# Writing three layers of a graph network as software pipelines in a fixed instruction order

## The chip, the cores and the metric

The kernel runs on one core of one Trainium2 chip. The time is the device time of the core in microseconds (us), median of several executions. "PE" is TensorE's matmul stream, "PEld" its weight loads, "DVE" VectorE, "ACT" ScalarE, "POOL" GpSimd, "SP" SyncE, which only issues transfers. The engines have one queue each and meet through semaphores.

## The reference, cut to what matters

Four graph layers over N = 3327 nodes with D = 512 features and a sparse adjacency; each is `x = layernorm(x + layer(x))`. The sum over neighbours is dense in the reference (`mask @ x`, or a masked softmax):

```python
# layer 0: attention, 8 heads of 64 columns
Wh = einsum('nd,hdo->hno', x, W);  f1 = Wh . a1;  f2 = Wh . a2
e = leaky_relu(f1[:, :, None] + f2[:, None, :], 0.2), masked by adj > 0
x = layernorm(x + elu(softmax(e) @ Wh))
# layer 1: mean over neighbours, two dense products, combined
out = relu(concat(x @ W_self + b_self, (mask @ x / deg) @ W_nb + b_nb) @ W_comb + b_comb)
# layer 2: mean over at most 64 neighbours
xj = leaky_relu(nb_mean @ W_nb.T + b_nb);  xi = leaky_relu(X @ W_line.T + b_line);  out = xi + xj
# layer 3: attention as in layer 0, 4 heads of 128 columns, W expanded as quaternions
```

## The kernel before

The 3327 rows are 26 blocks of 128. For each block the kernel first turns its rows of the adjacency into lists of edges, in chunks of 128 edges: 247 chunks in all, walked in 74 groups of up to four. A layer writes a table of transformed rows to DRAM. For each chunk GpSimd gathers 128 table rows with one indirect transfer (`gt`); VectorE makes a 128 x 128 matrix of zeros and ones that tells which edge belongs to which row (`sel`); TensorE multiplies the two and accumulates the block's sum in PSUM (`acc`). In the attention layers the gathered rows are first multiplied by the edge's weight for each head. After the last chunk of a block comes its end: bias, activation, residual, layernorm (its reciprocal root on GpSimd, `rs`), transposes, and the next layer's dense products.

```python
# attention, one block after the other (cut)
for l, c0, g, at in groups(b):
    G = gather(gp, self.table, l, c0, g, HM + H)
    S = select(sp, l.dst, c0, g)
    ...                                        # scores: one small product per chunk, exp on ScalarE
    for c in range(g):
        nc.vector.tensor_mul(Gh[:, c, :, :OUT], Gh[:, c, :, :OUT], w[:, c, :, None].to_broadcast([P, H, OUT]))
    for c in range(g):
        for s in range(2):
            nc.tensor.matmul(acc[:, s, :hh * M], S[:, c, :], G[:, c, s * hh * M:(s + 1) * hh * M], ...)
...                                            # block end
# layer 1, end of a block (cut)
nc.vector.scalar_tensor_tensor(y, acc, rdeg[b], zb, ALU.mult, ALU.add)
nc.vector.scalar_tensor_tensor(y, y, 0.0, xres[b], ALU.max, ALU.add)
layernorm(fin, y, x2)
xt = transposed(fin, ps, x2)
nc.vector.tensor_add(tb, times(ps, xt, wn2), bn);  store(t2_d, b, tb)
nc.vector.tensor_add(xi, times(ps, xt, wl2, "px"), bl)
...                                            # leaky relu, xres[b] = xi + x2
```

Here the order of instructions on each queue is not the order of this text: an automatic scheduler with a model of durations rearranges them.

## Time and profile before

| | before |
|---|---|
| median | 2683.0 us (4 executions, 2678.6 to 2690.4) |
| TensorE, VectorE, GpSimd busy | 78%, 52%, 40% |
| lengths of the five stages | 318, 827, 555, 496, 493 us |

The stages are cut at the first gather of each layer: projection and weights, then layers 0 to 3. This cut, and the lines under it, are in the prediction below. A row of the table of engines by stage reads: window, its length, then busy us (and number of instructions) of PE, PEld, DVE, ACT, POOL, then the granted TensorE clock as a share of full speed, the busy share of the DMA engines, and GB/s.

### The profile page before, as it was taken

Reading aid. Unit: us, or ns where it says so; the run is one execution under the profiler, and the core shown is the slowest. Engines: PE = TensorE matmul, PEld = TensorE weight load, DVE = VectorE, ACT = ScalarE, POOL = GpSimd, SP = SyncE. Lnnn points to the kernel's source line nnn. Section 1 sums busy time; section 2 is a strip of 40 time slices with the busy share of each in tenths; the row PEclk is TensorE's granted clock in tenths of the full one; section 3 lists DMA queues with packets and bytes.
Section 4 is the critical chain, followed back from the end, with each engine's and each line's share of the span. In section 5 each row is a group of like instructions: output and inputs, shape, how many; then the busy total and the mean of one; then the engine's idle time right before and its main releaser. Section 6 shows DMA issues by size and latency. Waiting matters only on the chain. (4 is left out here: it accounts for less than half of the span.)

```text
span 2688.7 us, 22997 instructions
## 1 busy us (share of the span) xinstructions
PE 2087.9 (78%) x6894; PEld 1234.9 (46%) x6894; DVE 1395.8 (52%) x4087; ACT 408.4 (15%) x913; POOL 1080.5 (40%) x1244
## 2 busy tenths in 40 slices
PE   6697667787878777777888888568888877777775
PEld 3453355565555555423333333123333346666654
DVE  8976155577777774312333443312223336677776
ACT  2124111112222211100000000000111121111111
POOL 1000253433232322176554441565645527556451
PEclk9798988888888887898998998889999988888777
DMA  6136254444554432266554441565544427556442
GB/s 217 61 132 199 72 145 118 118 129 148 166 155 154 140 106 85 65 195 185 157 153 147 139 140 44 151 189 155 163 126 138 142 80 208 153 157 170 134 143 61
DMA packets 127529, 372.23 MB, mean 138 GB/s; under 512 B 25642, under 2 KB 27178, under 8 KB 127396
## 3 DMA queue, kind: packets, MB, share of 16 engines
q0 software_dynamic: 79040, 262.10, 34.6%
q1 hardware_dynamic: 48356, 108.57, 11.8%
q8 instruction: 58, 0.95, 0.2%
q14 instruction: 75, 0.61, 0.1%
HBM read 329.38 MB, written 41.21 MB: 138 GB/s over the span
## 5 line engine op out<-in xcount | busy, mean ns | idle before, releaser
L801 POOL DMA_INDIRECT gt<-t_d,idx x988 | 984.7, 997 | 1024.3 <-issue 331.8
L911 PE MATMUL acc<-gt,sel 128*128 128x260 f32 (+1 forms) x1976 | 626.7, 477 | 250.1 <-DVE gt L907 104.4
L911 PEld LDWEIGHTS acc<-gt,sel 128*128 128x128 f32 x1976 | 456.6, 240 | 356.8 <-ACT gt L905 108.1
L1036 PE MATMUL acc<-gt,sel 128*128 128x512 f32 x988 | 491.7, 627 | 47.4 <-DMA gt<-t_d,idx 46.2
L907 DVE TENSOR_TENSOR gt<-gt,pe 128x512 f32<-128x512 f32 x494 | 317.8, 678 | 13.5 <-ACT pe L904 8.5
L1036 PEld LDWEIGHTS acc<-gt,sel 128*128 128x128 f32 x988 | 178.6, 196 | 284.5 <-issue 208.1
L808 DVE TENSOR_TENSOR sel<-lane,dst 128x384 f32<-128x384 f32 (+2 forms) x284 | 169.0, 595 | 233.5 <-PE acc L1036 142.8
L663 PE MATMUL po<-wn,xt 128*128 128x512 f32 x416 | 219.9, 677 | 7.2 <-ACT xt L657 6.9
L663 PE MATMUL po<-w,xt 128*128 128x512 f32 x416 | 209.3, 643 | 3.0 <-ACT xt L657 3.0
L657 ACT COPY xt<-pt 128x512 f32<-128x512 f32 x112 | 65.6, 586 | 892.6 <-PE pt L655 855.1
L891 ACT ACTIVATE ds<-place,nmid 128x384 f32<-128x384 int16 (+2 forms) x148 | 95.8, 650 | 529.9 <-PE pe L895 524.0
L655 PE MATMUL pt<-s_ident,xres 128*128 128x128 f32 x312 | 59.5, 321 | 120.4 <-DVE xres L674 107.7
L663 PEld LDWEIGHTS po<-wn,xt 128*128 128x128 f32 x416 | 89.8, 223 | 127.4 <-issue 101.1
L685 POOL MEMSET ab<- 128x1 int32 x26 | 2.7, 103 | 349.2 <-ACT m L691 340.8
L663 PEld LDWEIGHTS po<-w,xt 128*128 128x128 f32 x416 | 81.8, 207 | 121.4 <-issue 87.9
L716 DVE MAX8 cand<-val 128x8 f32<-128x832 uint16 (+41 forms) x259 | 127.7, 522 | 0.0
L655 PEld LDWEIGHTS pt<-s_ident,xres 128*128 128x128 f32 x312 | 41.8, 168 | 153.3 <-issue 103.4
L672 POOL TENSOR_SCALAR rs<-mv 128x1 f32<-128x1 f32 x104 | 22.5, 217 | 189.8 <-DVE mv L670 155.3
L663 PE MATMUL px<-wl,xt 128*128 128x512 f32 x208 | 95.7, 603 | 0.8 <-DVE tb L1073 0.8
L691 ACT ACTIVATE m<-ab 128x1664 bf16<-128x1664 int32 x52 | 82.7, 1590 | 80.6 <-DVE val L692 69.3
L663 PE MATMUL po<-wx,xt 128*128 128x512 f32 x208 | 94.6, 597 | 0.0
L674 DVE TENSOR_SCALAR xres<-e,mv,rs 128x512 f32<-128x512 f32 x52 | 30.0, 576 | 124.2 <-POOL rs L673 124.1
(178 smaller groups left out, 2023.8 us busy)
## 6 DMA issues: line engine op xcount, KB each, us to landing
ab<-in_adj_dram SPq DMA_DIRECT2D x25, 832.0 KB, 4.9
ab<-in_adj_dram SPq DMA_DIRECT2D x25, 831.5 KB, 6.1
gt<-t_d,idx POOLq DMA_INDIRECT x988, 3.7
t_d<-tb SPq DMA_DIRECT2D x50, 256.0 KB, 2.0
t_d<-tb SPq DMA_DIRECT2D x25, 264.0 KB, 2.2
t_d<-tb SPq DMA_DIRECT2D x25, 260.0 KB, 2.0
xres<-in_x_dram SPq DMA_DIRECT2D x25, 256.0 KB, 5.7
z_d<-zb SPq DMA_DIRECT2D x25, 256.0 KB, 3.5
```

The source lines that it names most:

```text
L655: nc.tensor.transpose(pt[:, c, :], src[:, c * P:(c + 1) * P], ident)
L657: nc.scalar.copy(xt, pt)
L663: nc.tensor.matmul(po, xt[:, c, :], w[:, c], start=c == 0, stop=c == DC - 1)
L674: nc.vector.tensor_scalar(o, y, mv[:, 0:1], rs, ALU.subtract, ALU.mult)
L691: nc.scalar.activation(m, ab, AF.Sign, accum_out=half[:, s:s + 1])
L716: nc.vector.max(out=top, in_=seg)
L801: nc.gpsimd.indirect_dma_start(out=t[:, c, :], out_offset=None, in_=table[:, :], in_offset=bass.IndirectOffsetOnAxis(ap=l.idx[:, c0 + c:c0 ...
L808: nc.vector.tensor_tensor(s[:, :g, :], lane1[:, None, :].to_broadcast([P, g, P]), which[:, c0:c0 + g, None].to_broadcast([P, g, P]), ALU.i ...
L891: nc.scalar.activation(ds[:, :g * P], place[:, c0 * P:(c0 + g) * P], AF.Abs, bias=l.nmid)
L907: nc.vector.tensor_mul(Gh[:, c, :, :OUT], Gh[:, c, :, :OUT], w[:, c, :, None].to_broadcast([P, H, OUT]))
L911: nc.tensor.matmul(acc[:, s, :hh * M], S[:, c, :], G[:, c, s * hh * M:(s + 1) * hh * M], start=at + c == 0, stop=at + c == last)
L1036: nc.tensor.matmul(acc, S[:, c, :], G[:, c, :], start=at + c == 0, stop=at + c == last)
```

## The change

Its intent is that TensorE never stands for a block's end. Every group and every block end becomes a generator that yields between stages; one step of the loop advances every live generator by one stage, the oldest first, so the stages of some four groups and two blocks are interleaved by hand. From layer 1 on the scheduler is switched off and the queues run in the order written. Cut to its core:

```diff
+class Stages:
+    def step(self):
+        for stages in list(self.live):
+            if next(stages, self) is self:
+                self.live.remove(stages)
...
+        def group(self, item, pools, accs, done):        # attention
+            G = gather(gp, self.table, l, c0, g, H * M)
+            ...
+            yield
+            S = select(sp, l.dst, c0, g)
+            ...                                           # ds, and the score products pe
+            yield
+            ...                                           # sc, exp
+            yield
+            nc.vector.tensor_mul(Gc[:, :, :OUT], Gc[:, :, :OUT], w[:, :g]...)   # one for the group
+            for c in range(g): ... nc.tensor.matmul(accs[b][s], S[:, c, :], G[:, c, ...])
...
+    ctx.enter_context(tc.manual_schedule())               # layers 1 to 3
...
+        def layer1_end(b, acc):
+            yield
+            ...                                           # y from acc, zb, xb; moments -> mv, rs
+            yield
+            scaled(x2, y, mv, rs)
+            xt = transposed(fin, ps, x2)
+            yield
+            nc.vector.tensor_add(tb, times(ps, xt, wn2), bn)
+            store(t2_d, b, tb, 2)
+            yield
+            xi = fin.tile([P, D], F32, name="xi")
+            nc.vector.tensor_add(xi, times(ps, xt, wl2), bl)
+            nc.vector.scalar_tensor_tensor(xi, xi, SAGE_ALPHA, xi, ALU.mult, ALU.max)
+            nc.vector.tensor_add(xres[b], xi, x2)
```

Besides this, the attention table keeps two score columns beside each head's features, so one operation adds both; the list making has fewer small operations; the residual x of layers 0 and 1 is reloaded from DRAM; the preparation of later weights goes into earlier pipelines; and buffers are handed on one by one and not at the ends of pools.

## The prediction

> **What bounds the kernel now.** I read the page first (TensorE 78% busy, VectorE 52%, no engine full), then cut the span at the first gather of each layer, because an average over five different stages says nothing. The table of engine busy time by stage:
>
> ```profile
> 0.00:318.00 318.00, 245.46 (x947) 134.33 (x947) 208.19 (x955) 84.60 (x154) 8.97 (x32) 0.88 0.40 133
> 318.00:1145.00 827.00, 627.70 (x2380) 447.28 (x2380) 523.39 (x1535) 170.84 (x381) 268.16 (x316) 0.83 0.44 129
> 1145.00:1700.00 555.00, 453.19 (x1014) 187.51 (x1014) 195.48 (x341) 15.24 (x26) 267.46 (x301) 0.92 0.47 142
> 1700.00:2196.00 496.00, 405.07 (x1071) 171.23 (x1071) 130.70 (x327) 51.28 (x88) 269.76 (x299) 0.93 0.49 145
> 2196.00:2689.00 493.00, 356.50 (x1484) 294.55 (x1483) 338.00 (x929) 86.41 (x266) 266.14 (x299) 0.79 0.53 148
> ```
>
> Columns: window, its length, then busy us of PE, PEld, DVE, ACT, POOL, then granted clock, DMA share, GB/s. Rows: projection and weights (318 us), layer 0 (827), layer 1 (555), layer 2 (496), layer 3 (493). Layers 0 and 3 are attention, 1 and 2 means over neighbours with dense products. No engine is over 82% in any of them, so order and waits, not work, cost the time. The timeline of layer 1 shows how:
>
> ```profile
> 1400.47 3.70 PE L663 MATMUL po<-wn,xt 128*128 128x512 f32 x8
> ...
> 1419.85 0.61 DVE L674 TENSOR_SCALAR x<-e,mv,rs 128x512 f32<-128x512 f32 x1 [3.96 <-POOL rs L673]
> ...
> 1420.61 1.08 PE L655 MATMUL pt<-s_ident,x 128*128 128x128 f32 x4 [3.36 <-DVE x L674]
> ...
> 1423.19 5.23 PE L663 MATMUL po<-wn,xt 128*128 128x512 f32 x8
> ```
>
> TensorE stood 3.36 us for a block's layernorm, and the same eight passes then took 5.23 us instead of 3.70: it pays for a gap twice, once standing and once at half clock. (The first passes after the gap start 0.85 us apart, warm ones 0.43.) The layer boundaries, and the pace of the gather and of VectorE's weighting, in the same view of other windows:
>
> ```profile
> 317.73 1.18 POOL L801 DMA_INDIRECT gt<-t_d,idx  x1 [67.76 <-DMA t_d<-bias]
> ...
> 1699.68 1.00 POOL L801 DMA_INDIRECT gt<-t_d,idx  x1 [31.64 <-DVE wa L943]
> ...
> 2402.49 3.68 DVE L907 TENSOR_TENSOR gt<-gt,pe 128x512 f32<-128x512 f32 x6
> ...
> 2403.09 0.95 POOL L801 DMA_INDIRECT gt<-t_d,idx  x1 [0.30 <-issue]
> ```
>
> The first attention gather waited 67.76 us for weight products of layer 1 that it does not use; layer 2's waited 31.64 us, the end of it for layer 3's weights. A gather costs POOL 0.95 + 0.30 = 1.25 us a chunk, whatever it waits for. In layer 3 the table of waits carries the same point as layer 1:
>
> ```profile
> PEld acc L911 <- DVE gt L907: 98.8, 58, 6.8
> ```
>
> **What the Trainium skill says.** "TensorE: Matmul & The Clock Gate", Part 1: after an idle window of about 3.4 us the clock halves, and about 3.4 us of sustained work restores it. The trace agrees: 0.85 against 0.43 us a pass after a 3.36 us gap. The section "Back-to-back issue gap" there gives about 216 ns for 512 warm columns; here an f32 product is two records of 0.43 us, so 0.86 us, and the trace decides. "VectorE: DVE Perf Modes", Mode 1x: one f32 result per cycle at 0.96 GHz, so 0.53 us for 512 columns; six products in 3.68 us are 0.60 us each, leaving some 0.07 us to save for every instruction merged away. "DMA: Bandwidth & Descriptors", Issuing engine by pattern: indirect transfers belong to GPSIMD, so the 1.25 us per chunk stays on POOL; the change does not touch it.
>
> **The change, part by part.** The lists hold 42 chunks in block 0 (three lists of 14) and 19, 15, 13, 11, 10, 10, 9, 9, 8, 8, five 7s, eight 6s, two 5s: 247 chunks in 74 groups a layer (988 gathers and 148 activations on the page agree). Per block of L chunks and n groups, warm:
> POOL: 1.26 L + 1 (two small layernorm operations, 0.2 + 0.56 plus gaps), sum 337.
> PE, layer 1: 0.86 L + 7.4 (transposes 0.5, two dense products of 8 x 0.43). PE, layer 2: 0.86 L + 5.7 (one product 3.44, scores 0.9, column mean 0.86, transposes 0.5).
> PE, attention: 1.1 L (four passes of 0.22 for the sum, two of 0.1 for the scores).
> DVE, attention: 0.45 n + 0.73 L + 3.7 (selection 0.06 + 0.13 a chunk, comparison 0.13 + 0.07, scores 0.2, merged weighting 0.06 + 0.53; block end 3.7).
>
> Layers 1 and 2. Each block's tail is cut into stages one group apart, with the sums of later groups between them, so TensorE no longer stands for the layernorm. Taking the larger of PE and POOL block by block gives 416 us for layer 1 (53 of them block 0, where gathers set the pace) and 377 for layer 2. PE alone would be 405 and 361. To each I add start and tail, since the next layer's gathers need every row of the table: some 15 us and 25 us (finishing the scores), and some 20 us for waits that remain: 450 and 420. The preparation of layer 3's weights, some 14 us of VectorE at the end of layer 1 (eight pairs of 0.69 each, and copies), moves into the middle, where VectorE is 35% busy. Saving 105 + 76.
>
> Layer 3. POOL 337, DVE 311, PE 272; larger of them by block 343. All three are close, and POOL must stop for each block's variance before it gathers on, so I expect 50 us of coupling and ends: 395, saving 98. Inside DVE's sum: 494 products become 148 instructions, two layers x 173 x 0.07 = 12 us each; three score operations become two, 74 x 0.16 = 12 us each.
>
> Layer 0 stays with the automatic scheduler, but its order of emission is now staged too. PE work warm: 247 x 1.1 = 272, dense 26 x 7.4 = 192, list products some 40, together 504 where 628 were busy at clock 0.83. DVE: 523, less 24 for attention, less some 30 for the list operations (about eight per list of 0.14 us busy and two per group of slots: 8 x 22 x 0.14 + 5), plus two more structures at some 13 us (fewer fit before the first gather): 495. Two engines near 500 need luck to finish under 600; I take 680, 73% of PE, against 61% of it (504 of 827) now. ACT takes over the copies (41 evacuations and four small operations per list, some 40 us) and has room at 171 of 827. Saving 147.
>
> Projection and weights. PE needs 26 x 5.7 = 147 plus eight weight products and the bias, some 40. They now lie in one pipeline instead of one after the other. Score weights must come first (eight pairs of 0.69 us, 11 us, after a load of 9), so 20 + 187 + finish and first gather 15 + 10 for closing the started structure + some 8 of gaps = 240, saving 78.
>
> Residuals of layers 0 and 1 in DRAM add two stores and loads of 256 KB a block, at 45 to 50% DMA share beside other work: nothing on the path. The final checks go into layer 3's pipeline: 10 us of tail, in its figure.
>
> Sum: 240 + 680 + 450 + 420 + 395 = 2185.
>
> **The rivals.** (1) POOL becomes the bound: at 337 a layer it cannot beat the table above, but if each layernorm pair makes POOL stop some 3 us x 26, layers 2 and 3 lose 60 to 80 each and the end is 2330. For: POOL's waits for the mean and variance already run to 16 us. Against: five or six gather buffers are two groups of lead. (2) The fixed order puts a slow producer ahead of ready work, as a list scheduler would not; then layer 3 stays at 460 and layer 1 at 500: 2310. For: queues are in order. Against: stages are a whole group (3 to 5 us) apart, longer than most handoffs here. (3) Layer 0 is VectorE-bound with single buffers in its list pool and one bank for transposes and list products: 780, so 2290. For: DVE 523 of 827 is spread. (4) TensorE is warm throughout and layer 0 reaches 600: 2080.
>
> **Range.** All parts but layer 0 have waits that are seen and removable; a loss would need the gain of some 500 us to vanish in new waits. Rivals 1 and 3 together give about 2400, rival 4 with good coupling 2060. I state 2185 us, 8 in 10 between 2060 and 2350; faster by over 2% 0.96, same 0.03, slower 0.01.
>
> **What would show it.** The granted clock in layers 1 and 2 near 1 (0.92 and 0.93 now), TensorE's waits for the normalised row nearly gone, gathers of the first layers not waiting for a bias or for score weights, 148 weighting instructions of some 1.9 us, POOL over 75% busy in layer 3. I would be wrong if layer 3 stays above 450 with POOL standing for the variance, or if layer 0 keeps TensorE near clock 0.83 at over 780 us.

## The result, and the profile after

The changed kernel took 2294.4 us (median of 4, 2290.1 to 2298.7) against 2683.0 us, ratio 0.8549, 95% interval 0.8524 to 0.8574. It is clearly faster and inside the range, but 109 us above the number. The engines by stage, in the same columns and the same five stages as before:

```profile
0.00:271.50 271.50, 226.83 (x933) 126.50 (x933) 181.14 (x754) 81.99 (x162) 7.54 (x22) 0.99 0.41 130
271.50:907.50 636.00, 560.66 (x2418) 406.73 (x2419) 518.62 (x1244) 191.42 (x492) 277.85 (x303) 0.91 0.63 195
907.50:1458.90 551.40, 454.65 (x1047) 201.64 (x1045) 193.38 (x339) 20.29 (x35) 274.39 (x302) 0.91 0.53 160
1458.90:1861.00 402.10, 379.81 (x1069) 165.17 (x1069) 126.29 (x330) 47.98 (x81) 266.09 (x299) 0.99 0.61 179
1861.00:2293.50 432.50, 338.03 (x1484) 282.41 (x1484) 348.45 (x687) 81.05 (x246) 269.89 (x327) 0.84 0.59 169
```

| stage | before | predicted | after | after less predicted |
|---|---|---|---|---|
| projection, weights | 318 | 240 | 271.5 | +31 |
| layer 0 | 827 | 680 | 636.0 | -44 |
| layer 1 | 555 | 450 | 551.4 | +101 |
| layer 2 | 496 | 420 | 402.1 | -18 |
| layer 3 | 493 | 395 | 432.5 | +37 |

Layer 1 is the odd row. It was to lose 105 us and lost 4, with its clock still at 0.91, while layer 2, whose block ends are cut into stages too, runs at 0.99. The timeline of layer 1 after the change (start, duration, engine, line, operation, operands; in brackets the idle time of the engine just before and what ended it) shows what TensorE stands for:

```profile
1210.78 3.60 PE L711 MATMUL po<-wl,xt 128*128 128x512 f32 x8
...
1214.41 0.69 DVE L1242 TENSOR_TENSOR xi<-po,bl 128x512 f32<-128x512 f32 x1 [2.41 <-PE po L711]
1215.14 0.69 DVE L1243 SCALAR_TENSOR_TENSOR xi<-xi 128x512 f32<-128x512 f32 x1
1215.86 0.69 DVE L1244 TENSOR_TENSOR xres<-xi,x 128x512 f32<-128x512 f32 x1
1216.47 0.54 DVE L725 TENSOR_SCALAR x<-e,mv,rs 128x512 f32<-128x512 f32 x1
...
1217.16 1.08 PE L703 MATMUL pt<-s_ident,x 128*128 128x128 f32 x4 [2.79 <-DVE x L725]
```

The product with `wl` ends at about 1214.4. VectorE stood 2.41 us for it, then does three operations on it, and only then the `x` of the next block, whose inputs had long been there; TensorE, with nothing before the transposes of that `x` in its queue, stands 2.79 us. The same happens in nearly every block, as the table of waits in layer 1 says (engine, line, what it waited for: us in all, times, longest):

```profile
POOL rs L720 <- DVE mv L718: 179.9, 24, 13.8
...
PE pt L703 <- DVE x L725: 70.3, 25, 3.9
DVE neg L1207 <- DMA raw<-in_L_gnn_W_dram: 29.7, 1, 29.7
```

The other lines of before have these answers. The first gathers of layers 0 and 2 now wait 35.57 us for a list and 11.36 us for the last dense product. The six multiplies of 0.60 us became operations such as the third line, for four chunks at once:

```profile
271.45 1.40 POOL L871 DMA_INDIRECT gt<-t_d,idx  x1 [35.57 <-DVE cand L793]
...
1458.88 1.00 POOL L871 DMA_INDIRECT gt<-t_d,idx  x1 [11.36 <-PE po L711]
...
1965.06 2.27 DVE L971 TENSOR_TENSOR gt<-gt,w 128x2048 f32<-128x2048 f32 x1
```

The wait of the aggregation for the weighting in layer 3, 98.8 us in 58 waits, has no line of that name left. It is not gone, though; part of it stands under another name:

```profile
PEld acc L977 <- issue: 38.1, 42, 2.7
```

"Issue" means that the profile knows nothing that was waited for. But all 40 of these waits that are longer than 0.2 us end 0.07 us after the end of a weighting multiply (L971). So TensorE still stands some 38 us for the weighting.

### The profile page after: what moved, and what is told of

Read it like the earlier page. It is cut to its first block, busy times and chain, and to the rows that moved or that the text cites. A ratio compares the mean times of both kernels' runs of the same rounds, so it can differ in the third digit from the quotient of the medians.

```text
span 2293.5 us, 22330 instructions
## 1 busy us (share of the span) xinstructions
PE 1960.0 (85%) x6950; PEld 1182.5 (52%) x6950; DVE 1367.9 (60%) x3351; ACT 422.7 (18%) x1016; POOL 1095.7 (48%) x1251
## 4 chain that ended last, share of the span: by engine, by line
PE 38%; DVE 9%; DMA 5%; issue 4%; POOL 4%; ACT 1%; SPq 0%; POOLq 0%; DVEq 0%; ACTq 0%
PE acc L1163 16%; PE po L711 12%; PE acc L977 5%; DMA gt<-t_d,idx 4%; POOL gt L871 3%; PE pt L703 1%; PE pe L960 1%; PE pmean L907 1%; DVE h L991 1%; PE pf L893 1%; DVE xi L1243 1%; DVE xi L1242 1%; DVE h L996 1%; DVE x L725 1%; DVE gt L971 1%
## 5 line engine op out<-in xcount | busy, mean ns | idle before, releaser
L977 PE MATMUL acc<-gt,sel 128*128 128x264 f32 (+1 forms) x1976 | 553.9, 436 | 81.2 <-issue 73.5
L977 PEld LDWEIGHTS acc<-gt,sel 128*128 128x128 f32 x1976 | 415.3, 217 | 175.6 <-issue 90.8
L1163 PEld LDWEIGHTS acc<-gt,sel 128*128 128x128 f32 x988 | 192.0, 205 | 267.7 <-issue 205.3
L971 DVE TENSOR_TENSOR gt<-gt,w 128x1536 f32<-128x1536 f32 (+2 forms) x148 | 284.7, 1923 | 1.5 <-ACT w L967 1.3
L878 DVE TENSOR_TENSOR sel<-lane,dst 128x384 f32<-128x384 f32 (+2 forms) x284 | 167.7, 592 | 70.3 <-PE acc L1163 37.4
L711 PE MATMUL po<-wn,xt 128*128 128x512 f32 x416 | 195.7, 612 | 5.6 <-ACT xt L705 5.2
L1237 DVE TENSOR_TENSOR tb<-po,bn 128x512 f32<-128x512 f32 x26 | 18.0, 692 | 204.6 <-PE po L711 204.6
L779 DVE MAX8 cand<-val 128x8 f32<-128x832 uint16 (+39 forms) x259 | 124.3, 521 | 0.0
L703 PE MATMUL pt<-s_ident,x 128*128 128x128 f32 x208 | 38.1, 314 | 82.1 <-DVE x L725 70.8
L960 PE MATMUL pe<-g3fall,ds 128*128 128x8 f32 x494 | 64.8, 254 | 45.0 <-DVE ds L957 45.0
L960 PEld LDWEIGHTS pe<-g3fall,ds 128*128 128x128 f32 x494 | 68.4, 201 | 58.1 <-issue 43.2
L967 ACT ACTIVATE w<-sc 128x24 f32<-128x24 f32 (+4 forms) x148 | 28.2, 191 | 380.0 <-DVE sc L965 267.7
```

The lines of the kernel that those rows point to most:

```text
L703: nc.tensor.transpose(pt[:, c, :], src[:, c * P:(c + 1) * P], ident)
L711: nc.tensor.matmul(po, xt[:, c, :], w[:, c], start=c == 0, stop=c == DC - 1)
L779: nc.vector.max(out=top, in_=seg)
L878: nc.vector.tensor_tensor(s[:, :g, :], lane1[:, None, :].to_broadcast([P, g, P]), which[:, c0:c0 + g, None].to_broadcast([P, g, P]), ALU.i ...
L960: nc.tensor.matmul(pe[:, c], ds[:, c * P:(c + 1) * P], self.fall[:, H:, b], start=True, stop=True)
L971: nc.vector.tensor_mul(Gc[:, :, :OUT], Gc[:, :, :OUT], w[:, :g].rearrange("p c (h o) -> p (c h) o", o=1).to_broadcast([P, g * H, OUT]))
```

## The experiments

My theory after this reading: in a fixed order, a stage that holds a product and the operations of another engine on that product makes the other engine's queue stand for it, and everything behind, though ready, stands too. Rivals: GpSimd's stop for the variance, the 179.9 us above, starves the gathers; the reloaded residuals compete with the gathers; or the clock is a limit of its own.

Twelve kernels ran, in four sets, each set on one chip beside the kernel before. All gave correct results. The chip of the second and fourth sets is slower: the kernel before takes 2728 to 2729 us there against 2685 and 2690 us on the other two, and layer 2, which no edit but e4's touched, 433 to 442 us against 402 to 405. So I compare stages with unedited stages of the same set (where the first set has none, with the changed kernel above, whose layers 0 and 2 agree with those of e1 to e3 within 3 us). Where that chip loses time in layer 3, VectorE's waits for a group's score product and gathered rows show. This is the line of e6:

```profile
DVE sc L964 <- remote: 54.2, 12, 8.5
```

"Remote" is the profile's word for a release that it can assign to no instruction or transfer of the core. In e7 the line reads 53.2 us and in e8 59.7 us; no layer 3 on the other chips has one, and, which matters below, e12's has none either. Without it the unedited layers 3 of the second set would take some 429 and 435 us, as elsewhere.

Lengths of the stages in the profiled executions, edited stages in bold. They come from one execution each; e2's was the fastest of its six, 19 us under the median, and e7's the slowest of its five, 15 us over it:

| run | set | projection | layer 0 | layer 1 | layer 2 | layer 3 | median of all |
|---|---|---|---|---|---|---|---|
| e1_xi_later | 1 | 271.6 | 637.7 | **447.0** | 402.5 | 433.9 | 2193.7 |
| e2_scores_later | 1 | 268.5 | 637.7 | **537.5** | 401.6 | 417.7 | 2284.2 |
| e3_both | 1 | 269.6 | 638.5 | **441.7** | 403.8 | 431.5 | 2190.6 |
| e4_auto | 1 | 271.4 | 642.0 | **445.4** | **412.9** | **464.5** | 2237.3 |
| e5_newest_first | 2 | 271.1 | 646.9 | 558.0 | 437.5 | **742.2** | 2660.6 |
| e6_l0_unstaged | 2 | 271.5 | **705.7** | 557.8 | 433.3 | 483.5 | 2462.3 |
| e7_lists_later | 2 | **249.6** | **661.6** | 557.0 | 441.8 | 488.6 | 2385.5 |
| e8_weight_per_chunk | 2 | 270.9 | **659.3** | 559.5 | 435.4 | **471.6** | 2399.4 |
| c9_control | 3 | 273.4 | 638.6 | 551.5 | 402.8 | 435.3 | 2298.1 |
| e9_best | 3 | **272.8** | 638.8 | **441.3** | 404.0 | **421.7** | 2180.1 |
| e10_more_loads | 3 | **270.6** | **637.3** | **444.2** | 404.8 | **419.3** | 2181.7 |
| e12_vector_relief | 4 | **276.3** | 645.9 | **458.2** | 441.3 | **422.9** | 2245.8 |

**e1_xi_later: the operations on the product one stage later.**

```diff
-            nc.vector.tensor_add(xi, times(ps, xt, wl2), bl)
+            px = times(ps, xt, wl2)
+            yield
+            nc.vector.tensor_add(xi, px, bl)
```

> Only change: in layer 1 the three VectorE operations on wl2's product (bias, leaky relu, sum for layer 2's residual) are written one stage after the product, not in the stage of the product. Theory (a fixed order that puts them, waiting for their own product, ahead of the next block's scaled x makes TensorE wait for x, and the pass after the wait runs cold): TensorE's wait for x in layer 1, 70 us in 25 waits, falls below 15 us, layer 1 goes from 551 to 450-490 us, the whole from 2294 to 2200-2230, nothing else moves. Rival 1 (GpSimd's stop for the variance, 180 us in layer 1, starves the gathers): under 20 us. Rival 2 (residual reloads compete with the gathers for the DMA engines): under 20 us. Rival 3 (the granted clock alone): the gap goes but layer 1 stays above 530 us because the clock falls.

Measured: 2193.7 us (4 executions, 2192.7 to 2199.6), ratio to before 0.8173 (0.8143 to 0.8203) against 0.8549. Layer 1 by engines:

```profile
909.20:1356.20 447.00, 418.62 (x1047) 189.38 (x1045) 194.82 (x339) 20.29 (x35) 272.02 (x301) 0.97 0.65 197
```

And from its table of waits, GpSimd's for the variance and TensorE's for the normalised row:

```profile
POOL rs L720 <- DVE mv L718: 82.7, 21, 9.2
...
PE pt L703 <- DVE x L725: 5.4, 7, 2.9
```

One added `yield` took 104 us from layer 1 and changed the other stages by less than 2 us. The instructions are the same (339 on VectorE, 1047 on TensorE). TensorE's wait for `x` fell from 70.3 to 5.4 us, 65 us; and its busy time fell from 454.65 to 418.62 us, 36 us, because the passes after most of the waits no longer run cold: in the timeline of the changed kernel eight aggregation passes right after one wait took 5.25 us, eight dense ones later 3.60. 65 + 36 = 101 of the 104 us. The rivals fall, as the explanation of this gain: GpSimd's wait for the variance fell by 97 us without being touched. It was the effect, GpSimd ahead and standing for late statistics, not the cause. The clock rose to 0.97 by itself once TensorE had work. That VectorE's queue works strictly first in, first out is stated by the Trainium skill ("TensorE: Matmul & The Clock Gate", "Architectural detail: the array is 16x 32x32, not 1x 128x128"); this pair of runs agrees: `x`, ready behind `xi`, did not pass it.

**e2_scores_later: the weight preparation not ahead of the first selection.** The order also put the first VectorE operation of layer 3's weight preparation (the 29.7 us wait for its transfer, above) ahead of layer 1's first selection.

```diff
-        work.add(score_parts())
-        for item in groups():
+        parts3 = score_parts()
+        next(parts3)
+        for n, item in enumerate(groups()):
+            if n == 12:
+                work.add(parts3)
```

> Only change: layer 3's weight preparation in layer 1's pipeline keeps its load at the start, but its first operation on VectorE is written after 12 groups instead of in the second step, ahead of the first selection. Theory: VectorE's wait of 29.7 us for that load, with TensorE idle behind it at the start of layer 1, goes; layer 1 shortens by 18-28 us, the whole to 2266-2276. Rival (the start of layer 1 waits for the gathers or its own weights anyway): under 8 us.

Measured: 2284.2 us (6 executions, 2264.9 to 2291.6), 10 us less by the medians, with a spread larger than that; layer 1 is 14 us shorter in the profiled run, the fastest of the six. The expectation was too high. TensorE's first aggregation, first in the changed kernel, then here:

```profile
934.91 18.31 PE L1163 MATMUL acc<-gt,sel 128*128 128x512 f32 x36 [6.50 <-DVE sel L878]
```

```profile
926.33 1.09 PE L1193 MATMUL pt<-s_ident,raw 128*128 128x128 f32 x4 [3.60 <-DMA raw<-in_L_gnn_W_line_dram]
927.21 13.21 PE L1163 MATMUL acc<-gt,sel 128*128 128x512 f32 x25
```

With the selection early, TensorE's own queue still holds the transposes of layer 2's weights first, and those wait for their loads until 926.33. Only the 6.50 us and one later wait of 4.25 us were to be had, not VectorE's 29.7. I had read the wait of an engine that was not the last to be ready.

**e3_both: the two edits together.**

> Both edits together. Theory: they are of two separate times and add up: 90-125 us less, the whole 2170-2205, layer 1 430-465 us. If the clock takes it back or the gathers become the bound, less than 70 us together.

Measured: 2190.6 us (2182.6 to 2195.8), ratio 0.8158 (0.8122 to 0.8194): 104 us less than the changed kernel, 3 us less than e1 alone by the medians, 5 us in layer 1. As expected, in the lower half of the range; the second edit adds little.

**e4_auto: the same text, given back to the scheduler.**

```diff
-    ctx.enter_context(tc.manual_schedule())
```

> The changed kernel with the same code, but with layers 1 to 3 given back to the automatic scheduler (one line taken out). It measures what the fixed order itself is worth, in each layer. My theory: the fixed order wins in layers 2 and 3 (402 and 432 us stay below what the scheduler makes of them, by 20-60 us each) and costs in layer 1 (scheduler below 551 us, by 20-80). The whole 2280-2360. Rival (the whole gain of layers 1 to 3 comes from the fixed order): layers 1 to 3 go back to some 1545 us, the whole to 2440.

Measured: 2237.3 us (2236.0 to 2237.8), ratio 0.8329 (0.8301 to 0.8356), 57 us faster than the changed kernel. Layers 1, 2 and 3:

```profile
913.30:1358.70 445.40, 419.12 (x1047) 187.68 (x1045) 184.45 (x309) 20.29 (x35) 276.31 (x301) 0.98 0.62 192
1358.70:1771.60 412.90, 382.62 (x1069) 166.90 (x1069) 128.81 (x330) 50.55 (x82) 269.63 (x299) 0.97 0.60 174
1771.60:2236.10 464.50, 341.37 (x1484) 287.38 (x1484) 320.27 (x686) 85.60 (x245) 261.17 (x327) 0.82 0.55 157
```

The signs are as expected, two of the sizes and the whole are not. The fixed order is worth 10 us in layer 2 (20 to 60 expected) and 31 us in layer 3 (402.5 and 433.9 unedited in e1), and cost 106 us in layer 1 (20 to 80 expected), where the scheduler had moved the tail of a block back against the next: in its timeline an `x` is ready at 1194.9 us and its transposes start at 1205.19 us, without a wait. Against before (555, 496, 493 us) the same text under the scheduler gains 110, 83 and 28 us: as much in layer 1 as the fixed order mended by e1 (108), most of its gain in layer 2 (94) and half in layer 3 (59). That part comes from the staged text and what else the change did there, not from the fixed order.

**e5_newest_first: the other direction of a step, in layer 3.** `step` goes through `list(self.live)[::-1]`.

> The changed kernel, but in layer 3 each step goes through the live pipelines from the newest to the oldest: TensorE's score products stand before the aggregation products, and VectorE makes the next selection before it weights the oldest group. Theory (in layer 3 TensorE's waits for ds, 45 us, and what follows them at a low clock come from the order oldest first): layer 3 goes from 432 to 395-415 us, the whole to 2255-2280. Rival (VectorE, 348 busy of 432 us, is the bound and only start, end and its waits for gathers make up the rest): within 10 us either way.

Measured: 2660.6 us, ratio 0.9747 (0.971 to 0.9785). Layer 3 took 742.2 us where the unedited one of this set takes 483.5 and 488.6. Both the theory and the rival missed by far. The waits of layer 3:

```profile
DVE sel L883 <- PE acc L982: 299.3, 59, 6.8
```

My explanation is argued from the code and this line; no run with more buffers tests it. Selections have three buffers. Oldest first, a step first emits the product that frees a buffer and then the selection that takes it. Newest first, the selection comes ahead and wants the buffer whose product was emitted last in the step before, so VectorE stands for TensorE, then weights, then TensorE runs: the two engines take turns. If that is right, the order of a fixed pipeline and the count of its buffers are one choice, not two.

**e6_l0_unstaged: layer 0 without staging.**

```diff
-        work.add(g0.group(item, pools, accs, layer0))
         more()
+        for stage in g0.group(item, pools, accs, layer0):
+            pass
         work.step()
```

> The changed kernel, but in layer 0 all stages of a group are written together, as the kernel before wrote them, under the same automatic scheduler. Theory (layer 0's gain of 191 us is mostly the staging: gather, scores, weighting and products of four groups written side by side): layer 0 goes from 636 to 740-830 us, the whole to 2400-2490. Rival 1 (the gain comes from cheaper list operations and scores per head, with the order left alone): layer 0 stays under 680. Rival 2 (the merged weighting and the table's layout): the same, under 680.

Measured: 2462.3 us, ratio 0.9042 (0.9009 to 0.9074). Layer 0 is 705.7 us against 646.9 unedited (e5): 59 us. Staging the groups is worth less than I expected, even though the scheduler may reorder: it is a third of the layer's gain of 191 us (which is from another chip). The rest is not split up here beyond e8.

**e7_lists_later: TensorE's first 40 us.** In the changed kernel TensorE's queue had block 0's first list product early, and it stood 39.0 us for it.

```diff
             work.step()
-            more(2)
+            if t >= 3:
+                more(2)
```

> The changed kernel, but the list of block 0 goes on only from the fourth projection block, so that TensorE has three blocks' transposes and products in its queue ahead of the first list product, for which it now waits 39 us (the scheduler put that product early in TensorE's order). Theory (the projection stage is bound by TensorE, 227 busy of 271 us, and lost its first 40 us to that wait): projection 271 to 245-258 us, the whole 12-26 us less. Rival (VectorE's lists set the end of the stage, so a later start only moves the wait to the end, before the first gather): within 6 us either way or longer.

Measured: 2385.5 us, ratio 0.8745 (0.8724 to 0.8765). The projection stage fell to 249.6 us, as expected, but fewer lists were done by then, and layer 0 rose to 661.6: together 911.2 against 918.0 in e5. A saving of some 7 us, where 12 to 26 were expected of the whole; the list work had moved across the border.

**e8_weight_per_chunk: the weighting not merged.** The one multiply per group becomes a loop over its chunks.

> The changed kernel, but the features are weighted chunk by chunk again: 494 multiplies of 512 columns in place of 148 of up to four chunks, about 33 us more of VectorE over layers 0 and 3 going by the two profiles (317.8 against 284.7 us). Theory: layer 3 is bound by VectorE and takes all of its half, some 15 us; layer 0 has slack on VectorE (519 of 636 us) and takes 0-8. The whole 12-28 us more. Rival: hidden, under 5 us.

Measured: 2399.4 us, ratio 0.8798 (0.8774 to 0.8821). Against the unedited stages of the set, layer 0 is 12 us longer (659.3 against 646.9, where 0 to 8 were expected) and layer 3 is 12 to 17 us shorter (471.6 against 483.5 and 488.6). Layer 3, its VectorE 10 us busier:

```profile
1925.10:2396.70 471.60, 337.12 (x1484) 281.39 (x1484) 356.92 (x859) 81.26 (x246) 270.71 (x327) 0.83 0.54 155
```

My expectation failed for layer 3. The likely reason is that TensorE can start on the first chunk after 0.6 us and need not wait for the whole 1.9 us operation; a merge that saves VectorE's time lengthens the hand-over. The traces bear this out: the waits `PEld acc L977 <- issue` come to 6.2 us here, and to 34.6 and 35.2 us in the unedited layers of e6 and e7, and TensorE is busy 337 us for 355 and 353.

**c9_control, e9_best and e10_more_loads.** The control is the changed kernel unedited. The best version joins e3 with two more edits: lists that start late and catch up, and in layer 3 a stage between weighting and product, with the buffers that it needs.

```diff
+            if t >= 3:
+                more(3 if t < 9 else 2)
...
                                  w[:, :g].rearrange("p c (h o) -> p (c h) o", o=1)...)
+            if self.k == 1:
+                yield
...
-        pools = (pool_in(lay, "l3g", 6), pool_in(lay, "l3s", 3),
+        pools = (pool_in(lay, "l3g", 7), pool_in(lay, "l3s", 4),
```

The third loads each residual twice (`for r in range(2)` around the loads of layers 0 and 1).

> The changed kernel itself, unedited, as the control of this chip: the chip of the second set of runs was slower in stages that no edit touched (layer 2 433 to 442 us there, 402 on the first). On a chip like the first: 2285-2300 us. On one like the second: 2370-2410.

> Four edits in four different stages, to be read stage by stage against the control: in layer 1 the two of the first set (xi a stage later; layer 3's weight preparation after 12 groups); in the projection the list of block 0 starts with the fourth block and then catches up in threes; in layer 3 the aggregation product is written one stage after the weighting it reads, with a seventh gather buffer and a fourth selection buffer. Theory (a stage that holds a producer and its consumer on another engine makes the in-order queues wait): layer 3 20-45 us shorter, layer 1 100-115, projection 12-22, layer 2 unchanged, the whole 130-170 us below the control. Rival for layer 3 (VectorE or GpSimd is the bound): layer 3 within 8 us.

> The version before it, but every block's residual is loaded twice: x in layer 0, x1 and z1 in layer 1, so 78 more loads of 256 KB, 20 MB more. Theory (the reloads lie beside other work; DMA engines are busy 0.65 of layer 1): each of the two layers within 6 us, the whole within 10. Rival (they compete with the gathers now that layer 1 is bound by TensorE and the gathers): layer 1 15-40 us longer.

Measured: control 2298.1 us (2294.6 to 2303.3), ratio 0.8546 (0.8507 to 0.8585), as on the first chip. Best version 2180.1 us (6 executions, 2176.5 to 2186.1), ratio 0.8112 (0.8082 to 0.8142): 118 us below the control, less than the 130 to 170 I expected. With doubled loads 2181.7 us, ratio 0.8122 (0.8084 to 0.8159). By stages: layer 1 551.5 to 441.3 us, confirmed on one chip. Projection unchanged: TensorE has its first work at 14.87 us and is busy 237 us, for 230 in the control, but stands later in the stage for the lists that now come late. Layer 3 435.3 to 421.7, 14 us, between theory and rival: TensorE's waits right behind the weighting went from 38 to 2 us, but those for `ds` rose from 44.2 to 71.6 us. Of the fixed order, the three executions with this stage (e9, e10, e12) took 419 to 423 us and four without it on the fast chips 431 to 435; but one without it, e2's, took 417.7, so 14 us are not more than one execution can vary. The doubled loads, 20 MB more, cost layer 1 3 us and layer 0 nothing (637.3 against 638.8), although layer 1's DMA share rose from 0.65 to 0.72: the reload is hidden, and the rival that blamed it falls. (Only the loads were doubled, not the store.)

**e12_vector_relief: less VectorE work in layer 3.** In e9's layer 3 VectorE is 84 to 94% busy, window by window, from 103 us after its start to 39 us before its end. The edit weights the last chunk of groups of three or four on ScalarE, and forms the exponential linear unit as min(exp(h), 1) in the sum.

```diff
+            gv = g - 1 if self.k == 1 and g >= 3 else g
...
+            for h in range(H if gv < g else 0):
+                cols = G[:, gv, h * M:h * M + OUT]
+                nc.scalar.mul(cols, cols, w[:, gv, h:h + 1])
```

> The best version so far, with VectorE relieved in layer 3 alone: the last chunk of each group of three or four is weighted on ScalarE (four scalings of 128 columns), and the exponential linear unit takes the smaller of exp(h) and 1 in the sum (one operation of 0.45 us per block less). About 70 x 0.53 + 26 x 0.45 = 49 us of VectorE less of 346; ScalarE gains some 280 x 0.25 = 70 us on 81. Theory (once the products are a stage later, VectorE is the bound of layer 3's middle: 84 to 94% busy in its windows from 103 us on): layer 3 goes from 422 to 385-405 us. Rival (GpSimd's gathers and TensorE's low clock hold it): within 8 us of 420. On a chip as slow as the second set's: compare with its layer 3 of 471 to 487 us and its layer 2 of 433 to 442.

Measured: 2245.8 us (6 executions, 2240.5 to 2249.4), ratio 0.8222 (0.8198 to 0.8247), on the slow chip. Layers 2 and 3:

```profile
1380.40:1821.70 441.30, 385.08 (x1069) 168.57 (x1069) 125.77 (x331) 47.58 (x81) 264.05 (x299) 0.95 0.55 163
1821.70:2244.60 422.90, 328.10 (x1484) 273.89 (x1484) 299.28 (x660) 165.09 (x535) 314.37 (x327) 0.86 0.60 173
```

VectorE fell by 47 us (346 to 299), as worked out. Layer 3 took 422.9 us, the rival's figure and not the theory's 385 to 405. It is 61 to 66 us less than the unedited layer of this chip in the second set (483.5 and 488.6), but that comparison is not fair: 54.2 and 53.2 us of those are the "remote" waits told above, and this layer has none. What remains to compare with is e9's 421.7 us on another chip, and against that the relief gave nothing. VectorE's saved work came back as waits for gathered rows, 28.9 us in e9's layer 3 and here

```profile
DVE sc L964 <- DMA gt<-t_d,idx: 64.5, 30, 4.4
```

GpSimd has hardly a pause left: its gathers took 289.0 us (242.0 in e9; why they are slower is open), 81.7 us went by before them with nothing known to wait for (12.7 of it at once), and its waits for the variance fell from 67.6 to 22.8 us. So the traces speak for the rival, that the gathers hold the layer. No run of e9 on this chip makes that sure, and none relieves GpSimd.

## Why the prediction was right or wrong, point by point

Right: faster, in the range, and the mechanism. The mean layers lost time by the stops of TensorE and the cold passes after them; where the stops went, the clock went to 0.99 (layer 2; 0.97 in layer 1 with e1). Layer 2 had 402 us for 420, partly by errors that cancel: TensorE was busy 380 us, not 361, and stood 22 us where block 0's gathers, start, tail and waits had been given some 60.

**The step that failed is in layers 1 and 2: "Each block's tail is cut into stages one group apart, with the sums of later groups between them, so TensorE no longer stands for the layernorm", with the saving of 105 us for layer 1.** It is true of layer 2 and false of layer 1. I checked that stages are apart, not what each holds: layer 1's last stage holds a dense product and VectorE's use of it, and by the order oldest first that stands ahead of the next block's `x` in the same step. In layer 2 the dense products (`g3.products`) and their use (`g3.write`) were two stages from the start. The prediction had this as rival 2, with layer 1 at 500 us, and set it aside with "stages are a whole group (3 to 5 us) apart, longer than most handoffs here"; within a stage the distance is nothing. Layer 1 measured 551.4, with 70.3 us of TensorE's waits for `x`; with the stage split, 447.0 against the predicted 450. The whole kernel with only the two edits of layer 1 took 2190.6 us, 6 us from the predicted 2185, though errors of the other stages cancel in that.

**Projection, +31.** Two terms were mis-sized. The list products, "some 40", I booked in layer 0 alone. By the view by line they take 97 us, 61 of them in layer 0 and 36 in the projection: 3.26, 3.30, 3.21 and 26.57 us there; the last of these:

```profile
0.00:271.50 271.50, 26.57 (x200) 24.95 (x200) 0.99 0.41 130
```

187 + 36 = 223 us of TensorE, and 227 were measured. And TensorE's start was at 39 us, not 20, behind block 0's list. That the stage is 31 us over and not 55 is luck, an error that cancels: the 33 us of finish, closing and gaps shrank to some 6 (271.5 less 39 less 227). e7 and e9 show that curing the second alone gives little, as the lists must be made all the same.

**Layer 0, -44.** "73% of PE" (504 of 680 is 74%) was too cautious: the same 504 us are 79% of 636, and the measured busy time, which the list products and a clock of 0.91 make 561 us, is 88%. Of its gain, staging is 59 us (e6) and the merged weighting 12 us (e8), which is the figure predicted for it; VectorE was busy 519 us, not 495.

**Layer 3, +37.** Here the terms were too small. VectorE was busy 348, not 311 us: a block's end on it takes 4.8 us, not 3.7 (its nine rows in the profile sum to 124 us for 26 blocks). TensorE was busy 338, not 272, at a clock of 0.84. The 12 us expected from the merged weighting turned into its opposite here (e8). "POOL over 75% busy" reads 62% in the view (270 of 432.5 us), but 77% with the 63 us of short pauses between its gathers, which the prediction's 337 had counted. GpSimd's stops for the variance, rival 1, come to 80.4 us in this layer; what they delay is not told apart. That VectorE's work sets the middle of the layer, as I thought before e12, is not borne out: with 47 us less of it the layer was no shorter than e9's, and GpSimd's gathers are the likelier bound. How the 37 us divide among these terms stays open.

**Residuals in DRAM, "nothing on the path".** Right: doubling the loads cost 3 us at most. (The change adds two loads and one store a block, not two stores.)

What stays open: two thirds of layer 0's gain (cheaper lists, earlier buffers, weights moved away are not told apart); what the "remote" waits are that make one chip slower; what bounds layer 3; and why e2's layer 3, unedited, ran in 417.7 us at clock 0.88.

## What to carry to other kernels

In a hand-ordered pipeline, look at every stage that holds a product and another engine's use of it: where operations stand behind that use for which another engine waits, put a stage between them, and count one more buffer for what then lives longer. (Not each such stage costs: layer 1's `tb` shares one with its product and was left so. VectorE stands 136.2 us for it in e1, and the layer reached 447 us.) A long wait in a table may be the effect of another engine's lateness: follow the chain to the operation whose inputs were ready. And before taking a fixed order, run the same staged text under the scheduler: here the scheduler won one layer by 106 us and lost the other two by 41.

## What the Trainium skill lacked or had wrong

- "TensorE: Matmul & The Clock Gate", Part 1, gives one idle window of about 3.4 us, free-running, for the clock to halve. Here layer 1 of the changed kernel has sixteen waits of 2.79 us, as the profile shows them with modelled ends of matmuls; thirteen were followed by passes 0.85 us apart (warm 0.43) and three were not. So a somewhat shorter gap was not safe here.
- "DMA: Bandwidth & Descriptors", "Anatomy of one DMA - SWDGE (gpsimd) path", fits 2.0 us plus bytes over 436 KB per us, without saying whether indirect transfers follow it; by it I estimate 2.6 us for a gathered chunk of 256 KB. The median from issue to landing in the changed kernel is 3.8 us. GpSimd issues one such chunk every 0.95 + 0.30 us here.
- No page that I read says how far chips differ: the same kernel before took 2685 and 2690 us on two chips and 2729 on another, and the unedited layer 2 402 to 405 against 433 to 442 us. Stages must be compared on one chip.
